# Residual rows of one panel put together in DRAM ahead of time, in a two-layer graph attention kernel

## The chip, the cores and the metric

The kernel runs on one core of a Trainium2 chip. The metric is the device time of one execution in microseconds (us); lower is better. The core has a matrix engine (TensorE, PE in the profile; its weight loads are PEld), a vector engine (VectorE, DVE), an activation engine (ScalarE, ACT), GpSimd (POOL) and a sync engine (SP). In this kernel SP issues nearly all loads from DRAM, and POOL issues the stores and those transfers that add to what is already at their destination. All transfers (DMAs) run on the same 16 DMA engines.

## What is computed

Two layers of graph attention over N = 2708 nodes with D = 1024 features, each with a layer norm ahead and a residual. Layer 0 is the one that the change touches:

```python
h = jnp.maximum(_layernorm(x, axis=-1), 0.0)
f = h @ Wf + bf;  g = h @ Wg + bg
e = relu(f @ g.T)
attention = softmax(where(adj > 0, e, NEG), axis=1)
x = x + attention @ (h @ W + bW)              # layer 0
h = jnp.maximum(_layernorm(x, axis=-1), 0.0)
x = x + layer1(h, adj, W1, a1, a2)            # layer 1, attention from two dot products
```

The rows of a softmax sum to one, so the bias `bW` can be added to the result: layer 0 ends with `x + bW + (attention @ h) @ W`. The kernel computes it in this order. `x + bW` is what is called the residual here. The output of layer 0 is called `x1`.

## The kernel before

The nodes are cut into five panels of some 512 columns (`NP = 5`), and each panel into four tiles of 128 rows (tiles 16 to 19 are panel 4; a few left-over rows have two tiles of their own in other panels). The rows of a tile are not contiguous in `x`: a tile takes four blocks of 32 rows that lie 128 rows apart, because of how masks are transposed (`places`). Matrix products are done by a scheme of seven half-size products (Strassen), called M1 to M7 in code and text.

For each panel of layer 0 four stages follow each other on PE:

- `project_q(p)`: the query side of the panel.
- `scores(p)`: for ten pairs of tiles (`for q in range(NQ)`, line 1403) seven products each, with one operand (`As`) streamed from DRAM; DVE evicts the results, turns the adjacency into masks and keeps row maxima. The masks are stored by POOL.
- `aggregate(0, p)`: attention times `h`, with `hc` streamed from DRAM.
- `project(0, p)`: the result times `W`, with `w` streamed from DRAM. For the last panel it runs pair by pair (`by_pair=True`, line 1705), in the order M1, M5, M2, M6, M7, M3, M4 for each of its two pairs of tiles, and each product of eight matmuls loads its own 1 MB of `w`.

`project` loads the weights of its first two products, then calls the `start` of `finish0(p)` (line 1218). For each tile, `start` loads the residual: two halves of 512 columns, each from four blocks of 32 rows (`load_rows_of`, line 278), so eight loads of 64 KB a tile. Then POOL adds the bias to each half by a DMA that accumulates (line 1612), with a source that repeats the same row 128 times. For panel 4, a mask is loaded as well for each tile (line 1600). When a product is evicted, `go` adds the residual to it, stores the row to `x1_d` (a DRAM tensor per tile, in tile order, that layer 1 reads), and when both halves are there `rows_done` starts layer 1's row work: layer norm, dot products, row maxima.

What sets the order. `load` keeps SP's loads in the order of the program (line 139), so a load that waits for a buffer or for room in flight holds up those after it. Loads go to rotating buffers: a pool of 12 (`strm`, for `w`, `hc`, `As`, raw adjacency) and one of 54 (`slot`, for residual halves, masks, scores). Two helpers interleave small work with PE's: `behind(us)` takes pieces from a list as PE's time allows, among them `put_quarters` (load `hq`, four DVE operations on each, store), which prepares layer 1 during the late part of layer 0. Instructions that are not held in order are arranged when the program is built.

The order at the end of layer 0 is: scores of panel 4, `project(0, 3)`, `aggregate(0, 4)`, `project(0, 4)`, then layer 1.

Of the kernel before, what the change touches and what calls it, by code (L numbers as in the profile page):

```python
# [12 lines left out]
OP = mybir.AluOpType  # L13
# [5 lines left out]
P = 128  # L19
W = 512  # L20
# [37 lines left out]
def kernel(  # L58
# [66 lines left out]
    def slot(name, shape=(P, WX), dt=FP):  # L125
        return slots.tile(list(shape), dt, tag="slot", name=name)
# [10 lines left out]
    def load(o, i):  # L137
        for a, b in in_16(o, i):
            tc.keep_in_program_order(nc.sync.dma_start(a, b))
# [102 lines left out]
    def row_halves(name, from_stream=False):  # L242
        return halves(stream(name)) if from_stream else [slot(name)[:, :W] for _ in range(2)]
# [1109 lines left out]
    def scores(p, B):  # L1353

        w = width[p]
        h = w // 2
        lo, hi = slice(0, h), slice(h, w)
        fetch, convert, turn = makers[p]
        rb = slot("rb")
        if p == 0:  # L1360
            spread(rb, columns_of(p, r_[:, first_col[p]:]))
        else:
            row_on_all(rb, r_d[p], p)
        acc = slot("acc")
        S = [None] * NT
        rates = (0.6, 1.0, 0.65, 0.65, 0.65)
        lefts = {}

        def product(q, m, ps, start):
            n, i = P, BY_SCORES.index(m)  # L1370
            if i % 2 == 0:
                t = stream("As", (P, 2, NH, P))
                lefts[q] = t
                k = min(2, 7 - i)
                load(t[:, :k].rearrange("p m c j -> p (m c j)"),
                     hs_d[q][:, i:i + k].rearrange("p m c j -> p (m c j)"))
            for c in range(NH):
                nc.tensor.matmul(ps[:n, :h], lefts[q][:, i % 2, c, :n], B[m][c // 2][:, c % 2, :h],  # L1378
                                 start=(start and c == 0), stop=(c == NH - 1), skip_group_check=True)

        def finish(q, s, k):

            n, mk = once(q, k), mk_sb[p, q]
            nc.vector.scalar_tensor_tensor(s[:, :w], s[:, :w], 0.0, mk[:, k, :w], op0=OP.max, op1=OP.add)
            if q == 0 and k == 0:
                nc.vector.tensor_copy(acc[:, :w], s[:, :w])
            else:
                nc.vector.tensor_tensor(acc[:n, :w], acc[:n, :w], s[:n, :w], OP.max)
            if q in known:
                raise_max(p, q, k, mk[:n, k, :w])  # L1390

        def last(q, sb, Z, m1):

            n = P
            product(q, M4, Z, False)
            add(sb[:n, lo], Z[:n, :h], m1[:n, lo])
            finish(q, sb, 1)
            mk_sb.pop((p, q))
            behind(rate, True)

        nc.hold = ("vector",)
        left_over = None
        for q in range(NQ):
            n = P
            make_until(q + 2)
            rate = 1.3 if NQ - 1 not in made else rates[p]
            if q + 2 <= LEFT:
                fetch(q + 2)
            sa, sb = slot("Sa"), slot("Sb")
            S[pairs[q][0]], S[pairs[q][1]] = sa, sb  # L1410
            X, Y, Z = (bank(f"s{k}") for k in "xyz")
            m1, t = slot("sm1"), slot("st")
            product(q, M1, X, True)
            for s in (lo, hi):
                add(m1[:n, s], X[:n, :h], rb[:n, s])
            if left_over:
                left_over()
            product(q, M6, Z, True)
            add(t[:n, lo], Z[:n, :h], m1[:n, hi])
            behind(rate, True)  # L1420
            product(q, M5, Y, True)
            add(t[:n, hi], Y[:n, :h], m1[:n, hi])
            if q + 1 <= LEFT:
                convert(q + 1)
            behind(rate, True)
            product(q, M2, X, False)
            add(sa[:n, lo], X[:n, :h], rb[:n, lo])
            if q + 1 <= LEFT:
                turn(q + 1, 0)
            behind(rate, True)  # L1430
            product(q, M7, Z, False)
            add(sb[:n, hi], Z[:n, :h], t[:n, hi])
            if q + 1 <= LEFT:
                turn(q + 1, 1)
            behind(rate, True)
            product(q, M3, Y, False)
            add(sa[:n, hi], Y[:n, :h], t[:n, lo])
            finish(q, sa, 0)
            behind(2 * rate, True)
            left_over = lambda q=q, sb=sb, Z=Z, m1=m1: last(q, sb, Z, m1)  # L1440

        sm, st = slot("Sa"), slot("Sb")
        S[MONO], S[TINY] = sm, st
        X, Y, Z = (bank(f"s{k}") for k in "xyz")
        m1, zs = slot("sm1"), slot("sz")
        t = stream("As", (P, 2, NH, P))
        load(t.rearrange("p e c j -> p (e c j)"), hsl_d.rearrange("p e c j -> p (e c j)"))

        def part(ps, e, m, start):
            for c in range(NH):  # L1450
                nc.tensor.matmul(ps[:, :h], t[:, e, c], B[m][c // 2][:, c % 2, :h], start=(start and c == 0),
                                 stop=(c == NH - 1), skip_group_check=True)
        part(X, 0, M1, True)
        add(m1[:, hi], X[:, :h], rb[:, hi])
        left_over()

        for c in range(NH):
            for g, (e, m) in enumerate(((0, M1), (1, M2), (0, M5), (1, M3))):
                nc.tensor.matmul(Z[B32 * g:B32 * (g + 1), :h], tinyT[:, e, c], B[m][c // 2][:, c % 2, :h], start=(c == 0),
                                 stop=(c == NH - 1), skip_group_check=True)  # L1460
        nc.scalar.copy(zs[:, :h], Z[:, :h])
        part(X, 1, M2, False)
        add(sm[:, lo], X[:, :h], rb[:, lo])
        behind(rate, True)
        part(Y, 0, M5, True)
        part(Y, 1, M3, False)
        add(sm[:, hi], Y[:, :h], m1[:, hi])
        finish(LEFT, sm, 0)
        for s, pick in zip((lo, hi), picks):
            V = bank("sv")  # L1470
            nc.tensor.matmul(V[:, :h], pick, zs[:, :h], start=True, stop=True)
            add(st[:, s], V[:, :h], rb[:, s])
        finish(LEFT, st, 1)
        mk_sb.pop((p, LEFT))
        behind(rate, True)
        nc.hold = ()
        return S, acc
# [113 lines left out]
    def bias_of_W(o, n, k):  # L1591
        return bass.AP(tensor=bw.tensor, offset=bw.offset + o, ap=[[0, n], [1, k]])

    def finish0(p):
        xs, seen = {}, {}

        def start(ts):
            for t in ts:
                if p == NP - 1:
                    first_mask[t] = load_mask(0, *pair_of[t])  # L1600
                if t == TINY:
                    xs[t] = halves_of_tiny("x_res")
                    for e in range(2):
                        for ps, i in by_quarters(x, places[TINY][0][1], e):
                            load(xs[t][e][ps], i)
                        for g, (ps, _) in enumerate(by_quarters(x, 0, e)):
                            nc.gpsimd.dma_start(xs[t][e][ps], bias_of_W(e * W + g * P, NY, P), accum_op=OP.add)
                    continue
                xs[t] = row_halves("x_res", t == MONO)
                load_rows_of(t, xs[t], x)  # L1610
                for e in range(2):
                    nc.gpsimd.dma_start(xs[t][e], bias_of_W(e * W, P, W), accum_op=OP.add)

        def go(t, e, c):
            add(xs[t][e], c, xs[t][e])
            if t == TINY:
                for ps, o in by_quarters(x1_d[t], 0, e):
                    store(o, xs[t][e][ps])
            else:
                store(x1_d[t][:, e * W:(e + 1) * W], xs[t][e])  # L1620
            seen[t] = seen.get(t, 0) + 1
            if seen[t] == 2 and t == TINY:
                put(0.5, lambda: rows_of_tiny())
            elif seen[t] == 2:
                rows_done(t, xs[t])

        def rows_of_tiny():
            xs[TINY] = row_halves("x_res")
            for e in range(2):
                nc.gpsimd.memset(xs[TINY][e], 0.0)  # L1630
                for ps, _ in places[TINY]:
                    nc.gpsimd.dma_start(xs[TINY][e][ps], x1_d[TINY][:, e * W:(e + 1) * W])
            rows_done(TINY, xs[TINY])

        def join(t, e, c):
            add(xs[t][e], xs[t][e], c)
        return start, join, go
# [199 lines left out]
```

## Time and profile before

| | us |
|---|---|
| median of 3 runs | 3094.57 |
| lowest and highest | 3094.34, 3098.68 |
| the profiled execution, whole | 3099.78 |
| its span, first to last instruction | 3098.0 |
| PE busy | 3002.8 (97%) |
| DVE busy | 2070.7 (67%) |
| POOL busy | 506.3 (16%) |
| ACT busy | 463.2 (15%) |
| mean granted clock of PE | 0.989 |

The profile describes one execution, with all its times counted from the start of the span. PE is busy nearly throughout, so the table says little of where time can be had; one has to look for the few places where PE waits or has a lower clock. In the span, the stages that the text speaks of lie at: scores of panel 4, 1771 to 1902; `project(0, 3)` from 1902; the end of `aggregate(0, 4)` (products M7 and M4, named `gz` and `gv` after their accumulators) 2044 to 2085; `project(0, 4)` (accumulators `px`, `py`, `pz`, `pv`) from 2085.15; layer 1's first long product from 2160.91. The residual halves appear as `x_res`, the source of the bias as `in_L_gnn_bW_dram`, `x1_d` as `x_d`, the reordered operands of layer 1 as `hq`, and masks loaded again from DRAM as `maskl`.

The DMA engines moved 764.70 MB, 247 GB/s over the span. SP's queue (q1) took 62.0% of the 16 engines' time, POOL's (q0) 16.4%.

### The profile page before, as it was taken

To read this page: it belongs to the slowest core of one execution; us is meant where nothing else is said; L and a number is where in the kernel's file an instruction comes from. 1 tells how busy PE (TensorE), PEld (TensorE's weight loads), DVE (VectorE), ACT (ScalarE), POOL (GpSimd) and SP (SyncE) were. 2 spreads that over 40 slices of the span, in tenths; PEclk is the share of its full clock that TensorE was granted. 3 is DMA by queue.
4 is the path that set the end of the run, shared out by engine and by line. 5 is a ranking of instruction groups with operands and counts; after the bars stand their busy time and mean duration, and the time that the engine had idled before them with its cause. 6 is when DMAs were issued, how large, how long until landed. Compare 5 with 4: busy or idle time off the path is not lost.

```text
span 3098.0 us, 41680 instructions
## 1 busy us (share of the span) xinstructions
PE 3002.8 (97%) x14630; PEld 2298.1 (74%) x14630; DVE 2070.7 (67%) x4615; ACT 463.2 (15%) x817; POOL 506.3 (16%) x786
## 2 busy tenths in 40 slices
PE   8998999899999999999999999997999999999998
PEld 4576777657877588885888886783777969879694
DVE  5767693776651596716975277766968768887853
ACT  3420020010110101101011001301222121212200
POOL 1421101310011110214101001141202010020202
PEclk9999999999999999999999999998999999999999
DMA  6999967998565796758967577789667868888896
GB/s 225 291 257 254 301 247 253 309 274 229 178 238 153 217 260 223 244 158 241 278 199 255 164 217 234 237 266 350 229 216 249 274 202 296 287 269 294 264 297 246
DMA packets 448577, 764.70 MB, mean 247 GB/s; under 512 B 175776, under 2 KB 262592, under 8 KB 448368
## 3 DMA queue, kind: packets, MB, share of 16 engines
q1 hardware_dynamic: 393008, 598.31, 62.0%
q0 software_dynamic: 55360, 163.73, 16.4%
q8 instruction: 116, 1.90, 0.3%
q14 instruction: 93, 0.76, 0.1%
HBM read 627.95 MB, written 133.91 MB: 246 GB/s over the span
## 4 chain that ended last, share of the span: by engine, by line
PE 71%; DVE 11%; DMA 7%; issue 7%; SPq 2%; POOL 1%; ACT 1%; POOLq 0%; DVEq 0%; ACTq 0%
PE sz L1378 6%; PE gx L661 6%; PE gy L661 6%; PE gz L661 5%; PE gz L1067 5%; PE pz L1267 4%; PE sx L1378 4%; PE sy L1378 4%; PE px L1267 4%; PE py L1267 3%; PE gx L1067 3%; PE gy L1067 3%; PE M_ps L574 3%; PE qz L661 2%; PE qx L661 2%
## 5 line engine op out<-in xcount | busy, mean ns | idle before, releaser
L1378 PE MATMUL sz<-B,As 128*128 128x288 f32 (+2 forms) x1200 | 293.5, 394 | 11.8 <-DVE st L45 8.8
L1378 PEld LDWEIGHTS sz<-B,As 128*128 128x128 f32 x1200 | 227.8, 191 | 61.8 <-DVE st L45 12.7
L1378 PE MATMUL sx<-B,As 128*128 128x288 f32 (+2 forms) x800 | 199.6, 392 | 6.4 <-DMA As<-hs_d 4.4
L1378 PE MATMUL sy<-B,As 128*128 128x288 f32 (+2 forms) x800 | 199.3, 392 | 2.3 <-DMA As<-hs_d 2.3
L661 PE MATMUL gz<-Sa,hc 128*128 128x288 f32 (+2 forms) x800 | 189.2, 397 | 6.3 <-DMA hc<-hg_d 6.3
L661 PEld LDWEIGHTS gz<-Sa,hc 128*128 128x128 f32 x800 | 153.8, 193 | 40.1 <-DMA hc<-hg_d 6.8
L1378 PEld LDWEIGHTS sx<-B,As 128*128 128x128 f32 x800 | 151.3, 190 | 40.1 <-DMA As<-hs_d 3.7
L1378 PEld LDWEIGHTS sy<-B,As 128*128 128x128 f32 x800 | 152.0, 190 | 33.4 <-issue 2.7
L1067 PE MATMUL gz<-quarter,hc 128*128 128x128 f32 (+2 forms) x1344 | 168.8, 279 | 3.8 <-DVE gT L45 3.7
L143 POOL DMA_DIRECT2D out_dram<-x_res x180 | 89.0, 501 | 482.1 <-DVE x_res L45 474.7
L1067 PEld LDWEIGHTS gz<-quarter,hc 128*128 128x128 f32 x1344 | 160.6, 191 | 5.1 <-DVE gT L45 4.6
L1267 PE MATMUL px<-w,gT 128*128 128x512 f32 x320 | 143.9, 602 | 7.5 <-DMA w<-in_L_gnn_W_dram 6.0
L1267 PE MATMUL pz<-w,ps 128*128 128x512 f32 x320 | 142.1, 594 | 0.8 <-DVE pt L45 0.8
L1267 PE MATMUL py<-w,ps 128*128 128x512 f32 x320 | 142.0, 593 | 0.0
L143 POOL DMA_DIRECT2D mk_d<-mask x55 | 35.8, 652 | 534.8 <-DVE mask L45 528.1
L1267 PEld LDWEIGHTS px<-w,gT 128*128 128x128 f32 x320 | 60.9, 193 | 80.9 <-issue 74.7
L1267 PEld LDWEIGHTS pz<-w,ps 128*128 128x128 f32 x320 | 60.2, 190 | 77.1 <-issue 70.7
L1267 PEld LDWEIGHTS py<-w,ps 128*128 128x128 f32 x320 | 60.5, 190 | 75.8 <-issue 73.9
L574 PE MATMUL M_ps<-wgT,wfT 128*128 128x512 f32 x256 | 113.5, 600 | 1.6 <-ACT hsT L45 1.6
L661 PE MATMUL gy<-T,hc 128*128 128x288 f32 (+2 forms) x480 | 111.6, 394 | 0.0
L977 POOL TENSOR_TENSOR gT<-gT,rr 128x2304 f32<-128x2304 f32 (+5 forms) x12 | 44.4, 3700 | 382.4 <-DVE rr L45 179.8
L661 PEld LDWEIGHTS gy<-T,hc 128*128 128x128 f32 x480 | 91.2, 190 | 19.5
(377 smaller groups left out, 5803.6 us busy)
## 6 DMA issues: line engine op xcount, KB each, us to landing
hc<-hg_d SPq DMA_DIRECT2D x175, 512.0 KB
As<-hs_d SPq DMA_DIRECT2D x150, 512.0 KB
hc<-hr_d SPq DMA_DIRECT2D x119, 512.0 KB
hc<-hs_d SPq DMA_DIRECT2D x112, 512.0 KB
w<-wt_d SPq DMA_DIRECT2D x96, 512.0 KB
w<-in_L_gnn_W_dram SPq DMA_DIRECT2D x72, 512.0 KB
md<-md_d SPq DMA_DIRECT2D x56, 512.0 KB
adj_i<-in_adj_dram SPq DMA_DIRECT2D x200, 128.0 KB
```

What stands on the lines that cost most here:

```text
L143: nc.gpsimd.dma_start(a, b)
L574: nc.tensor.matmul(ps, wfT[a][c // NH][:, c % NH, :], wgT[b][c], start=(c == 0), stop=(c == NC - 1))
L661: nc.tensor.matmul(ps[d], left(m, k, d), right(m, k), start=(start and k == 0), stop=(k == K - 1), skip_group_check=True)
L977: nc.gpsimd.tensor_tensor(of(e, s), of(e, s), by(s, k), OP.mult)
L1067: nc.tensor.matmul(ps[:, d], lhs[:, d * P:(d + 1) * P], inner_right(m, n, k), start=(start and k == 0 and d == 0), stop=(k == NK - 1), ski ...
L1267: nc.tensor.matmul(ps, left[i][m][:, k, :], w_[k], start=(start and k == 0), stop=(k == NH - 1), skip_group_check=True)
L1378: nc.tensor.matmul(ps[:n, :h], lefts[q][:, i % 2, c, :n], B[m][c // 2][:, c % 2, :h], start=(start and c == 0), stop=(c == NH - 1), skip_g ...
```

## The change

For panel 4 alone the residual is put together in DRAM during the scores of panel 4, some 300 us ahead of its use, and in the order of the tile. At pair 2 POOL issues four DMAs that copy the rows of `x` for tiles 16 to 19 into `x1_d`, DRAM to DRAM, 512 KB each, with the source as 4 groups of 32 rows. At pair 6 it issues four accumulating DMAs of 512 KB that add the bias row to all 128 rows of each tile in DRAM. In `project(0, 4)`, `start` then has two loads of 128 x 512 a tile from `x1_d` in place of eight loads and two accumulating DMAs. The later stores to `x1_d` are as before, over the same rows.

```diff
@@ -1406,6 +1406,8 @@
             if q + 2 <= LEFT:
                 fetch(q + 2)
+            if p in ORDERED and q in (2, 6):
+                (copy_residual if q == 2 else bias_residual)(p)
             sa, sb = slot("Sa"), slot("Sb")
@@ -1591,6 +1593,30 @@
+    def tiles_of(p):
+        return list(full(p)) + ([MONO, TINY][p - 1:p] if p in (1, 2) else [])
+
+    ORDERED = (NP - 1,)
+
+    def by_gpsimd(o, i, **k):
+        tc.keep_in_program_order(nc.gpsimd.dma_start(o, i, **k))
+
+    def copy_residual(p):
+        for t in tiles_of(p):
+            if t < MONO:
+                r = places[t][0][1]
+                by_gpsimd(x1_d[t].rearrange("(g r) c -> g r c", g=P // B32),
+                                    bass.AP(tensor=x.tensor, offset=x.offset + r * D, ap=[[P * D, P // B32], [D, B32], [1, D]]))
...
+
+    def bias_residual(p):
+        for t in tiles_of(p):
+            n = NY if t == TINY else P
+            by_gpsimd(x1_d[t], bass.AP(tensor=bw.tensor, offset=bw.offset, ap=[[0, n], [1, D]]), accum_op=OP.add)
+
@@ -1607,6 +1633,10 @@
                 xs[t] = row_halves("x_res", t == MONO)
+                if p in ORDERED:
+                    for e in range(2):
+                        load(xs[t][e], x1_d[t][:, e * W:(e + 1) * W])
+                    continue
                 load_rows_of(t, xs[t], x)
                 for e in range(2):
                     nc.gpsimd.dma_start(xs[t][e], bias_of_W(e * W, P, W), accum_op=OP.add)
```

The new POOL DMAs are held in program order on POOL; the loads from `x1_d` go through `load` and so keep their place on SP.

## The prediction

> **What bounds the kernel now.** I read the page first: TensorE (PE) is busy 97% of the 3098.0 us span, so only a place where PE stands idle or runs slowly can pay. Among the costly groups one line has a transfer behind its idle time:
>
> ```profile
> L1267 PE MATMUL px<-w,gT 128*128 128x512 f32 x320 | 143.9, 602 | 7.5 <-DMA w<-in_L_gnn_W_dram 6.0
> ```
>
> Its last columns are the idle time before these matmuls, 7.5 us, of which 6.0 ended with a load of weights `w`. I looked for those 6 us in the timeline of PE and found them in the last projection of layer 0, where the touched `finish0(4)` is in use:
>
> ```profile
> 2088.59 3.60 PE L1267 MATMUL py<-w,ps 128*128 128x512 f32 x8
> 2098.14 6.29 PE L1267 MATMUL px<-w,gT 128*128 128x512 f32 x8 [5.96 <-DMA w<-in_L_gnn_W_dram]
> 2104.27 3.60 PE L1267 MATMUL pz<-w,ps 128*128 128x512 f32 x8
> ```
>
> Columns: start, extent, what, idle time before and what ended it. PE stops for 5.96 us, and the next eight matmuls take 6.29 us instead of 3.60. Why `w` is late stands in the timeline of SP, which issues all loads in program order:
>
> ```profile
> 2054.56 2.82 SPq L139 DMA_DIRECT2D w<-wt_d  x2
> 2057.47 1.45 SPq L139 DMA_DIRECT2D maskl<-mk_d  x1
> 2058.97 7.89 SPq L139 DMA_DIRECT2D x_res<-in_x_dram  x8
> 2067.05 0.34 SPq L139 DMA_DIRECT2D maskl<-mk_d  x1
> 2067.84 5.95 SPq L139 DMA_DIRECT2D x_res<-in_x_dram  x8
> ...
> 2080.83 7.90 SPq L139 DMA_DIRECT2D x_res<-in_x_dram  x8
> 2088.77 1.82 SPq L139 DMA_DIRECT2D w<-in_L_gnn_W_dram  x2
> ```
>
> Between the weights of the second product (M5) and of the third (M2) stand 32 loads of 64 KB, the residual rows of panel 4. They hold SP from 2058.97 to 2088.73; M2's weights leave at 2088.77 and PE needs them at 2092.19. The bias then gets in their way: GpSimd (POOL) adds it by eight accumulating transfers.
>
> ```profile
> 2082.09 5.38 POOL L1612 DMA_DIRECT2D x_res<-in_L_gnn_bW_dram  x6
> 2089.75 0.86 POOL L1612 DMA_DIRECT2D x_res<-in_L_gnn_bW_dram  x1 [2.28 <-DMA x_res<-in_x_dram]
> 2095.24 0.86 POOL L1612 DMA_DIRECT2D x_res<-in_L_gnn_bW_dram  x1 [4.63 <-DMA x_res<-in_x_dram]
> ```
>
> The table by windows shows the DMA engines full (share 1.13 in 2089 to 2093, 1.09 in 2093 to 2098) at only 226 and 261 GB/s, against 402 in 2105 to 2120 without them. M2's weights, 1 MB, take 9.2 us.
>
> **What the Trainium skill says.** Its page "DMA: Bandwidth & Descriptors", section "Rules for kernel authors", calls small transfers mostly overhead and says to coalesce them. The trace agrees in kind: SP waits for an earlier `x_res` load to land 16 times, 6.6 us, in this stretch, so few bytes are in flight. The same page, "Queues, rings and completion order", says that each DMA engine takes turns between queues packet by packet. The trace agrees: in 2059 to 2067 POOL's queue moved 595 packets and SP's 492. "TensorE: Matmul & The Clock Gate", Part 1, halves the clock after an idle window of about 3.4 us; here the granted clock is 0.61 in 2098 to 2105. The DMA page again, "Why a DMA increments its semaphore by 16 and not by 1", says that a DMA takes as many engines as divide the slowest dimension of both sides: the new copies have a slowest dimension of 4, so perhaps 4 engines. No run here shows that yet.
>
> **The change part by part.**
>
> *SP in the last projection.* 32 loads of 64 KB become 8 of 256 KB; the four mask loads and the bytes (2 MB) stay. Alone, 12 issues would take some 12 x 0.4 = 5 us (an issue takes 0.31 to 0.42 when nothing holds it). But landing limits them: SP's queue moved 1.02 MB in 2059 to 2067, 126 GB/s, beside POOL's. At that rate 2 MB + 0.6 MB of masks take 21 us, and M2's weights leave at about 2080 at the latest. At the same rate 1 MB takes 8 us: 2088, and POOL's other traffic ends at 2083, which makes it earlier. Needed at 2092.2: margin 4 us or more. Their buffers hold no load back: the stream pool has 12, M2's two were last read by the M7 products, over at 2065. M6, M7 and M3 follow as the `gv` products free buffers (2068 to 2085), each before its use.
>
> *What goes.* PE idles 5.96 us less. The eight slow matmuls go from 6.13 us start to start (2098.14 to 2104.27) to 3.44: 2.69 less. Sum 8.65 us. The eight accumulates go from this stretch too; they held over half of the DMA engines (56.6% for POOL's queue in 2089 to 2105), about 9 us of the whole set there. That pays for the compression of the stage: from 2092 on PE takes 1 MB of weights per 3.44 us, 305 GB/s, which the 402 GB/s of 2105 to 2140 cover with stores and masks beside it.
>
> *What is late next.* VectorE's (DVE) eviction of M6 before M7 accumulates on it, 0.78 us at 2107.9, stays. After the stage the path is DVE's (layer norm, dots, row maxima; PE waits 8.33 us at 2151.58 for `mx`). It starts with the last products, so it moves forward whole. A hidden gain: DVE's 2.45 us wait for the bias at 2092.21 goes, worth nothing because PE stood.
>
> *What is added in scores 4.* Four DRAM to DRAM copies of 512 KB at pair 2, four accumulates of 512 KB at pair 6. On POOL: 8 instructions of 0.7 to 2.2 us (stores 0.73, accumulates 0.84 to 2.25), behind them only mask stores, one per 12.09 us, for which nobody waits in this stage. The accumulates wait for the copies, issued four pairs (48 us) earlier. Cost on POOL: nothing; uncovered, at most 16 us of POOL alone.
>
> On the DMA engines: the trace has no DRAM to DRAM transfer. From below nothing, since the engines are busy 0.65 to 0.82 here and PE never waits for `As`. From above: the eight accumulates of panel 3 were issued in 1890.9 to 1902.2 and the slowest landed in 15.8 us, so 2 MB took at most 27 us; twice that, 54 us, for DRAM on both sides. I take nothing, because loads run ahead:
>
> ```profile
> 1742.09 6.34 SPq L139 DMA_DIRECT2D As<-hs_d  x3
> 1771.20 1.89 PE L1378 MATMUL sx<-B,As 128*128 128x256 f32 x8
> ```
>
> The first `As` is issued 29 us ahead of its use; SP waits for PE to free buffers, so the lead persists, and a burst has to delay loads by over 20 us to be seen. The later `x_res` loads wait for accumulates about 200 us old: nothing.
>
> *Sum.* -8.65 + 0 = -8.6 us. The profiled execution took 3099.78 us (span 3098.0 and 1.8 around it); it would take 3091.2. It lies 5.2 above the median of the runs, so I put the difference on the median: 3094.57 - 8.6 = 3086.0.
>
> **The rivals.**
>
> *A, the stall goes:* 3086.0; its own range 3083 to 3088.3.
>
> *B, a new wait takes part of its place.* Bigger loads put more packets of SP beside POOL's `hq` loads, for which DVE already waits in turn (four waits, 6.0 us; PE lost 0.97 us at 2064.98 behind it). Those four waits grown by half are 3 us, and a wait for M6's or M7's weights at full rings could be 1 to 2. Against it: POOL's queue is free after 2083. Saving 4: 3090.6.
>
> *C, slower: the DRAM accumulates are slow.* Place: from pair 6 (issued about 1842) to the projection of panel 3. Its own bias accumulates are issued at 1890.9 on the same queue, and DVE uses the first at 1912.84. The point: 2 MB must take longer than about 54 us, twice the measured bound, so that they end after 1896 and push panel 3's 27 us past 1912.84. At three times the bound (81 us, end 1923) panel 3's bias lands up to 27 us later; DVE and PE stop some 20, and 2.7 more go to the clock: 3094.57 - 8.65 + 22.7 = 3108.6. For it: accumulates already ran at half speed. Against: four transfers can overlap.
>
> *D, the order of issue shifts.* Only held instructions keep program order; the others are put in order at build time by expected readiness, which changes here. Place: the DVE chain of 2138 to 2160, where each half dot costs 0.76 us (0.68 and 0.08). Twelve of them ahead of the maxima cost 9.1 and end the gain: 3095.1.
>
> *E, it does more.* The 9 us of freed DMA time also shorten other waits: 3081.
>
> **How the numbers follow.** Chances: A 0.48, B 0.18, C 0.07, D 0.22, E 0.05. I can tell 0.2%, 6.2 us, from no change: the bounds are 3088.4 and 3100.8. A, less 0.03 for its edge, and E lie below: faster 0.50. B, that edge and the lighter third of D (0.08) lie between: same 0.29. C and the rest of D (0.14), which has no bound in the trace and which I spread up to 15 us over its 3095.1, lie above: slower 0.21. The predicted time is A's, 3086.0. The range goes from 3082, which leaves out E, to 3103, which leaves out C and half of D's slower part (0.07): 0.19 outside.
>
> **What would show it.** Right: SP shows 8 `x_res` loads before M2's weights, issued by 2080 on the old clock; PE has no idle time before the third product and its matmuls take 0.43 us each; POOL has no L1612 there; scores 4 still spans 130.7 us (1771.2 to 1901.9). Wrong: a wait for `As` or `x_res` at 1840 to 1915 (C), a longer wait for `hq` (B), or a longer way from the last product to the first of layer 1 than the 17.7 us of now (2143.25 to 2160.91, D).

## The result and the profile after

| | before | after |
|---|---|---|
| median of 20 runs each, same chip, us | 3095.03 | 3087.0 |
| lowest and highest, us | 3092.05, 3104.18 | 3081.28, 3097.34 |
| the profiled execution, us | 3099.78 | 3084.88 |
| its span, us | 3098.0 | 3083.0 |
| data moved, MB | 764.70 | 766.79 |

The ratio is 0.9972, 95% interval 0.9964 to 0.998: 8.7 us less, 6.2 to 11.1; the two medians differ by 8.0. In the page's costliest groups, the line that led to the stall now reads (columns as before: busy time, mean ns, idle time before):

```profile
L1267 PE MATMUL px<-w,gT 128*128 128x512 f32 x320 | 141.2, 593 | 1.5 <-ACT pt L45 1.5
```

The 6.0 us behind a load of `w` are gone, and the busy time is 2.7 us lower, since the eight matmuls at the low clock are gone too. PE's timeline after, where the last projection begins (start, extent, what):

```profile
2083.55 3.60 PE L1267 MATMUL py<-w,ps 128*128 128x512 f32 x8
2086.98 3.60 PE L1267 MATMUL px<-w,gT 128*128 128x512 f32 x8
2090.41 3.60 PE L1267 MATMUL pz<-w,ps 128*128 128x512 f32 x8
2093.85 1.02 PE L1267 MATMUL py<-w,ps 128*128 128x512 f32 x2
2094.80 3.70 PE L1267 MATMUL pz<-w,ps 128*128 128x512 f32 x8
```

The second line is M2: no idle time, 3.60 us. Two matmuls of M3 now stand between M6 and M7 (the fourth line) and fill the 0.78 us in which PE waited for DVE there. SP's timeline after, in the same stretch:

```profile
2049.54 2.82 SPq L139 DMA_DIRECT2D w<-wt_d  x2
...
2053.99 1.35 SPq L139 DMA_DIRECT2D x_res<-x_d  x2
...
2066.21 1.15 SPq L139 DMA_DIRECT2D x_res<-x_d  x2
...
2068.89 2.33 SPq L139 DMA_DIRECT2D w<-in_L_gnn_W_dram  x2
```

Eight loads of 256 KB in pairs, the last at 2066.21, and M2's weights leave at 2068.89, 18 us before their use. The last column of the table by windows, after, is GB/s; the one ahead of it is the busy share of the DMA engines:

```profile
2084.00:2088.00 4.00, 4.00 (x11) 1.85 (x10) 2.11 (x5) 0.34 (x1) 0.00 (x0) 1.00 1.03 407
2088.00:2093.00 5.00, 5.00 (x14) 2.13 (x13) 1.99 (x3) 0.00 (x0) 0.57 (x1) 1.00 1.04 397
```

Before, while `w` was late, the same columns read:

```profile
2089.00:2093.00 4.00, 3.18 (x8) 1.14 (x6) 1.55 (x4) 0.37 (x1) 0.86 (x1) 1.00 1.13 226
2093.00:2098.00 5.00, 0.00 (x0) 0.00 (x0) 1.20 (x2) 0.00 (x0) 0.86 (x1) 0.86 1.09 261
```

The engines are as full as before, but carry 400 GB/s in place of 226 to 261.

The spans differ by 15.0 us, which is more than the change brought. By stages: 5.23 us lie ahead of the change's first instruction (scores of panel 4 begin at 1765.97, before 1771.20), mostly in small waits of the first 600 us, which the change does not touch; the profiled execution of before lay 5 us above its median. Scores of panel 4: 130.70 to 130.91, 0.21 longer. `project(0, 3)` with `aggregate(0, 4)`: 183.25 and 183.23. `project(0, 4)`, from its first product's start to its last product's: 54.50 to 44.83, 9.67 shorter (5.96 + 2.69 + 0.78 for the M6 wait, 0.24 left unexplained). From the end of that last product to the first long product of layer 1: the same 17.7 us. The remaining 0.3 us lie in layer 1. So the change's own places give 9.67 - 0.21 = 9.5 us, within the interval of the timed runs.

### The profile page after: what moved, and what is told of

The parts are those of the page before. It is cut to its first block, busy times and chain, and to the rows that moved or that the text cites. A ratio compares the mean times of both kernels' runs of the same rounds, so it can differ in the third digit from the quotient of the medians.

```text
span 3083.0 us, 41611 instructions
## 1 busy us (share of the span) xinstructions
PE 3000.3 (97%) x14630; PEld 2299.3 (75%) x14630; DVE 2069.9 (67%) x4615; ACT 460.9 (15%) x815; POOL 504.1 (16%) x786
## 2 busy tenths in 40 slices
DMA packets 447808, 766.79 MB, mean 249 GB/s; under 512 B 175488, under 2 KB 262304, under 8 KB 447568
## 4 chain that ended last, share of the span: by engine, by line
PE 74%; DVE 11%; issue 7%; DMA 5%; POOL 1%; SPq 1%; ACT 1%; POOLq 0%; DVEq 0%; ACTq 0%
PE sz L1378 6%; PE gx L661 6%; PE gy L661 6%; PE gz L661 5%; PE gz L1067 5%; PE sx L1378 4%; PE pz L1267 4%; PE px L1267 4%; PE sy L1378 4%; PE py L1267 3%; PE gy L1067 3%; PE gx L1067 3%; PE gv L661 3%; PE M_ps L574 3%; PE qz L661 2%
```

## Experiments

The open question was the cause of the stall. The change does two things at once in the last projection: SP issues 8 loads in place of 32, and POOL's eight accumulates are gone. And it adds 4 MB of written data in an earlier stage, which the timed result can't price. "Project" below is the same stretch of `project(0, 4)` as above: 54.50 us before, 44.83 after. All ratios are to the kernel before, beside it on the same chip.

| run | ratio, 95% interval | project, us |
|---|---|---|
| e1_copy_only | 0.9994, 0.9985 to 1.0002 | 53.51 |
| e2_small_loads | 0.9970, 0.9962 to 0.9978 | 45.69 |
| e3_split | 1.0007, 0.9998 to 1.0015 | 59.32 |
| e4_dram_work_alone | 1.0003, 0.9993 to 1.0012 | 54.24 |
| e5_plain_broadcast | 0.9993, 0.9985 to 1.0002 | 50.32 |
| e6_distinct_rows | 0.9997, 0.9988 to 1.0006 | 55.39 |
| e7_no_bias | 0.9973, 0.9965 to 0.9982 | 45.69 |
| e8_three_doses | 1.0064, 1.0049 to 1.0078 | 44.82 |
| e9_copy_plain | 0.9976, 0.9966 to 0.9985 | 44.88 |
| e10_spread | 0.9962, 0.9951 to 0.9973 | 44.83 |
| e11_two_panels | 1.0027, 1.0017 to 1.0037 | 44.83 |
| e12_two_spread | 0.9986, 0.9979 to 0.9993 | 44.82 |

### e1_copy_only: only the loads coalesced

The copies stay at pair 2; the accumulates stay in the last projection, on POOL.

```diff
-            if p in ORDERED and q in (2, 6):
-                (copy_residual if q == 2 else bias_residual)(p)
+            if p in ORDERED and q == 2:
+                copy_residual(p)
...
                     for e in range(2):
                         load(xs[t][e], x1_d[t][:, e * W:(e + 1) * W])
-                    continue
-                load_rows_of(t, xs[t], x)
+                else:
+                    load_rows_of(t, xs[t], x)
```

> Copies into x1_d at pair 2 as in the change and two loads of 256 KB a half tile row block from there, but the bias is added in the on-chip tiles by eight accumulating DMAs in the last projection, as before. Theory S (the third product's weights were late because SP stood behind 32 small loads): they leave SP some 15 us earlier, PE's 5.96 us wait and the 2.7 us of low clock go, 8 to 9 us below before. Rival T (the accumulates, which hold over half of the DMA engines, made them late): most of the wait stays, at most 3 us below before.

Measured: 0.9994, no gain that can be told. SP issues M2's weights early, in its timeline:

```profile
2072.43 2.30 SPq L139 DMA_DIRECT2D w<-in_L_gnn_W_dram  x2
```

and still PE stops, two products later. PE's timeline of the same run:

```profile
2093.57 3.60 PE L1267 MATMUL pz<-w,ps 128*128 128x512 f32 x8
2102.99 2.05 PE L1267 MATMUL py<-w,ps 128*128 128x512 f32 x2 [5.82 <-DMA w<-in_L_gnn_W_dram]
```

These matmuls are M3's. Its weights left SP at 2080.68, 22 us before, and landed as PE resumed. The accumulates were issued from 2080.21 to 2088.96, and this is the table by windows while they run:

```profile
2091.27:2095.27 4.00, 4.00 (x10) 1.72 (x9) 0.29 (x1) 0.00 (x0) 0.00 (x0) 1.00 1.09 273
2095.27:2099.27 4.00, 1.90 (x5) 0.57 (x3) 3.10 (x6) 0.00 (x0) 0.55 (x1) 1.00 1.09 270
```

A full share at 270 GB/s, much as before. SP's order alone does not make the stall: with the order mended, it moved to later weights.

### e2_small_loads: only the accumulates moved

All is as in the changed kernel, but the residual comes from `x1_d` in 32 loads of 64 KB, as many as before.

```diff
-                        load(xs[t][e], x1_d[t][:, e * W:(e + 1) * W])
+                        for ps, _ in places[t]:
+                            load(xs[t][e][ps], x1_d[t][ps, e * W:(e + 1) * W])
```

> Residual and bias put together in DRAM as in the change, no accumulate in the last projection, but fetched from there by 32 loads of 64 KB. Theory S: SP still stands behind the 32 loads until about 3 us before PE needs the third product's weights; without the accumulates these land in 3 to 5 us and not 9.2, so PE waits 0 to 3 us: 5 to 8 us below before. Rival T: all of the gain, and M2's weights in time however late they leave: 8 to 9 us below before, with no wait of PE.

Measured: 0.997, the whole gain. SP's timeline:

```profile
2077.16 5.20 SPq L139 DMA_DIRECT2D x_res<-x_d  x8
2082.41 0.94 SPq L139 DMA_DIRECT2D w<-in_L_gnn_W_dram  x2
```

PE's timeline:

```profile
2088.52 3.60 PE L1267 MATMUL px<-w,gT 128*128 128x512 f32 x8
```

M2's weights leave 6.1 us before their use, behind the same 32 loads, and arrive in time. In the kernel before they left 3.4 us before their use and needed 9.2. The M6 wait of 0.78 us is there again, which is most of what e2's stretch is longer than the changed kernel's. This pair of runs takes the two halves of the change apart: the coalesced loads alone bring nothing, the moved accumulates alone bring everything.

### e3_split: the second pair's residual asked for later

In the kernel before, the second pair's loads (and so its four accumulates) are put after the first pair's M6.

```diff
+        in_two = l == 0 and by_pair
-        start_of([t for g in todo for t in g[:2]] + ([other] if other else []))
+        start_of(list(todo[0][:2]) if in_two else [t for g in todo for t in g[:2]] + ([other] if other else []))
...
+                if in_two and m == M6 and j + 1 < len(todo):
+                    start_of(list(todo[j + 1][:2]))
```

> The kernel before with no work in DRAM: the residual rows of the second pair of tiles are asked for after the first pair's fourth product, so that 16 small loads and not 32 stand ahead of the third product's weights; all eight accumulates stay in the last projection. Theory S: weights leave SP at about 2074 on the clock of before, wait and low clock go: 8 to 9 us below before. Rival T: the accumulates still hold the engines: at most 3 us below before.

Measured: 1.0007. M2 has no wait any more, but six others have come, of 0.34 to 4.40 us, 9.9 in sum. The longest, in PE's timeline:

```profile
2124.00 4.41 PE L1268 MATMUL pz<-w,ps 128*128 128x512 f32 x6 [4.40 <-DMA w<-wt_d]
```

This run does not tell the two causes apart, since it moves both. Sixteen small loads now hold SP ahead of M7's weights, which leave at 2091.99 and are wanted at 2093.98; and four accumulates, issued from 2095.12, lie beside the weights of the second pair. It shows that asking for the second pair later, within the projection, gains nothing.

### e4_dram_work_alone: the added work without the benefit

The copies and the four large accumulates go into tensors that nobody reads; the last projection is that of before.

```diff
+    spare_d = {t: dram.tile([P, D], FP, name=f"spare_d{t}") for t in full(NP - 1)}
...
-                by_gpsimd(x1_d[t].rearrange("(g r) c -> g r c", g=P // B32),
+                by_gpsimd(spare_d[t].rearrange("(g r) c -> g r c", g=P // B32),
-            by_gpsimd(x1_d[t], bass.AP(...), accum_op=OP.add)
+            by_gpsimd(spare_d[t], bass.AP(...), accum_op=OP.add)
...
-                if p in ORDERED:
-                    for e in range(2):
-                        load(xs[t][e], x1_d[t][:, e * W:(e + 1) * W])
-                    continue
```

> The kernel before plus the four copies and four accumulates in DRAM during the scores of panel 4, into tensors that nobody reads. Theory S: hidden by the loads that run ahead, 0 to 0.5 us above before, with SP held for some 15 us after pair 6 and no wait of PE for As. Rival (the added work has a price that the measured gain already contains): 2 to 5 us above before.

Measured: 1.0003, interval 0.9993 to 1.0012, so the work costs between -2 and 4 us; the profile shows no wait for `As`, and the old stall at M2 (6.66 us). The work is hidden, as closely as this can be told: the interval does not rule out its rival's 2 to 4 us, but no wait in the profile would account for them.

### e5, e6 and e7: what it is in the accumulates

Three edits of the kernel before, for panel 4 alone: a plain DMA of the same bytes in place of the accumulate (e5), an accumulate of zeros from 128 different rows in place of one row repeated (e6), and no bias DMA at all (e7).

```diff
 e5
+     if p == NP - 1:
+         nc.gpsimd.dma_start(xs[t][e], bias_of_W(e * W, P, W))
+     else:
          nc.gpsimd.dma_start(xs[t][e], bias_of_W(e * W, P, W), accum_op=OP.add)
 e6
+ zero_d = dram.tile([P, W], FP, name="zero_d")
...
+     nc.gpsimd.dma_start(xs[t][e], zero_d if p == NP - 1 else bias_of_W(e * W, P, W), accum_op=OP.add)
 e7
+     if p < NP - 1:
          nc.gpsimd.dma_start(xs[t][e], bias_of_W(e * W, P, W), accum_op=OP.add)
```

> The kernel before, but for panel 4 the eight bias DMAs of the last projection overwrite the residual in place of adding to it: the same bytes from the same repeated row, at the same time, without the accumulate. It leaves the residual x out of panel 4's rows. Theory R (the source that repeats one row 128 times makes these transfers slow): the wait for weights stays, within 2 us of before. Theory C (the accumulate itself makes them slow): most of the wait goes, 6 to 9 us below before.

> The kernel before, but for panel 4 the eight accumulating DMAs read 128 distinct rows of a DRAM tensor of zeros in place of one repeated row. It leaves the bias out of panel 4. Theory R: the transfers run at the rate of other loads, the wait for weights goes, 6 to 9 us below before. Theory C: the accumulate costs what it did, within 2 us of before.

> The kernel before with the eight bias DMAs of the last projection left out (the bias is not added in panel 4), and no work in DRAM; the 32 small loads stay. It is the bound for every way of taking the accumulates away: 8 to 9 us below before. If the work in DRAM during the scores has a price of its own, this lies below the changed kernel by that price; expected 0 to 1 us.

Measured. e7, 0.9973: M2's weights left SP 6.6 us before their use, and PE did not wait. First SP's timeline, then PE's:

```profile
2085.84 0.94 SPq L139 DMA_DIRECT2D w<-in_L_gnn_W_dram  x2
2092.40 3.60 PE L1267 MATMUL px<-w,gT 128*128 128x512 f32 x8
```

This is the bound on what moving the bias can bring, and the changed kernel reaches it. e6, 0.9997: the stall is there in full, in PE's timeline:

```profile
2096.51 6.41 PE L1268 MATMUL px<-w,gT 128*128 128x512 f32 x8 [6.73 <-DMA w<-in_L_gnn_W_dram]
```

and the windows of e6 have the low rate at a full share:

```profile
2086.00:2090.00 4.00, 3.78 (x9) 1.33 (x7) 1.62 (x4) 0.58 (x1) 0.86 (x1) 1.00 1.12 227
2090.00:2094.00 4.00, 0.00 (x0) 0.00 (x0) 1.73 (x3) 0.00 (x0) 0.81 (x1) 1.00 1.10 262
```

So the repeated source row is not what makes them slow. e5, 0.9993: half of the wait remains (and one of 1.00 us comes later), in PE's timeline:

```profile
2092.81 3.92 PE L1267 MATMUL px<-w,gT 128*128 128x512 f32 x8 [2.92 <-DMA w<-in_L_gnn_W_dram]
```

Its weights left SP at 2084.14, behind the 32 loads and 5.75 us before they were wanted. The project stretch is 4.2 us shorter than before, but no gain shows in the timed runs, whose interval ends at 0.9985, 4.6 us; neither expectation was fully met. Plain bytes at that place still cost something where the weights leave late.

### e9_copy_plain: coalesced loads and a plain bias

e1 with e5's edit: the weights leave early, the bias moves the same bytes at the same place, and only the accumulation is missing.

```diff
 (on top of e1)
-                    nc.gpsimd.dma_start(xs[t][e], bias_of_W(e * W, P, W), accum_op=OP.add)
+                    if p == NP - 1:
+                        nc.gpsimd.dma_start(xs[t][e], bias_of_W(e * W, P, W))
+                    else:
+                        nc.gpsimd.dma_start(xs[t][e], bias_of_W(e * W, P, W), accum_op=OP.add)
```

> The run with copies alone (8 large loads from x1_d, bias DMAs in the last projection), but these bias DMAs overwrite in place of adding, for panel 4; it leaves the residual x out of panel 4's rows. If the accumulate is what fills the DMA engines and the late issue on SP only decides where it is felt, weights that leave early and no accumulate together give all of the gain, 7 to 9 us below before, with under 1 us of waiting for weights in the last projection. If 2 MB of any transfer there is too much, at least 3 us of waiting stays and it is at most 5 us below before.

Measured: 0.9976, project 44.88, no wait. The table by windows, while the bias moves:

```profile
2083.34:2087.34 4.00, 4.00 (x11) 1.84 (x10) 3.62 (x6) 0.36 (x1) 1.57 (x3) 1.00 1.03 412
2087.34:2091.34 4.00, 4.00 (x11) 1.77 (x10) 0.75 (x3) 0.23 (x1) 0.54 (x1) 1.00 1.04 372
```

Against e1's 273 and 270 GB/s, with the accumulation as the only difference of the two programs. That the transfers accumulate is what costs e1 its gain. Beside e5, which has the same plain bias, this run differs by the eight large loads (and the copies they read): there coalescing took the last waits away, 50.32 to 44.88 us.

### e8_three_doses: how much of the added work is hidden

Eight more accumulates of 512 KB at pair 6 of panel 4 (12 in place of 4), into tensors of their own that are cleared during scores of panel 3.

```diff
+        for i in range(2):
+            for t in range(F):
+                by_gpsimd(spare_d[i][t], bass.AP(...), accum_op=OP.add)
```

> The changed kernel with twice as much again added at pair 6: eight more accumulates of 512 KB in DRAM, into tensors that nobody reads (cleared by 16 stores in the scores of panel 3). If one dose of 2 MB takes 18 us of full DMA engines and hides behind loads that run 29 us ahead, three take some 54 us, the lead is used up, and PE waits for As or for panel 3's residual 10 to 30 us: 2 to 22 us above before. If accumulates in DRAM are cheap beside other loads, PE does not wait and it stays at the changed kernel's time.

Measured: 1.0064; by the two ratios 28.5 us above the changed kernel ((1.0064 - 0.9972) x 3095). Scores of panel 4 take 160.44 us in place of 130.91. SP's timeline of e8:

```profile
1840.93 44.94 SPq L139 DMA_DIRECT2D adj_i<-in_adj_dram  x8
```

PE's timeline of e8:

```profile
1892.48 3.78 PE L1378 MATMUL sx<-B,As 128*128 128x256 f32 x8 [27.41 <-DMA As<-hs_d]
```

The work that costs next to nothing in one dose stops PE for 27.41 us in three. The place shows in the changed kernel too. Its SP timeline at pair 6:

```profile
1836.96 19.58 SPq L139 DMA_DIRECT2D adj_i<-in_adj_dram  x8
1856.63 4.29 SPq L139 DMA_DIRECT2D As<-hs_d  x8
```

In the kernel before, the same eight loads of raw adjacency held SP for 5.14 us:

```profile
1842.19 5.14 SPq L139 DMA_DIRECT2D adj_i<-in_adj_dram  x8
```

In the changed kernel, in 1838 to 1856, POOL's queue took 84.2% of the DMA engines for 2.62 MB, and SP's 15.0% for 0.34 MB. So the `As` behind them left 14.4 us later, and the first was needed at 1861.04. Timeline of PE's weight loads, after:

```profile
1861.04 1.59 PEld L1378 LDWEIGHTS sx<-B,As 128*128 128x128 f32 x8 [0.34 <-DMA As<-hs_d]
```

The idle time ahead of it, 0.34 us, ended with `As`; between the groups before and after it there are 0.02 to 0.03 us. The stage is 0.21 us longer than before. So the cover was used up, and a little more.

### e10_spread: the accumulates apart

One large accumulate at each of the pairs 4 to 7, in place of four at pair 6.

```diff
+            if p in ORDERED and q == 2:
+                copy_residual(p)
+            if p in ORDERED and 4 <= q < 8:
+                bias_residual(p, [full(p)[q - 4]])
...
+    def bias_residual(p, ts):
+        for t in ts:
```

> The changed kernel with its four accumulates in DRAM issued one a pair, at pairs 4 to 7, and not all at pair 6. The loads of the scores stage should be held some 4 us at a time in place of 14 at once, so that As lands well ahead of use. If the one dose at pair 6 sometimes makes PE wait (its As landed just in time in the profile), this is 0.5 to 3 us below the changed kernel; if it never does, the same within 0.5 us.

Measured: 0.9962, interval 0.9951 to 0.9973; scores of panel 4 take 130.70 us, as before the change. SP's timeline:

```profile
1840.56 8.81 SPq L139 DMA_DIRECT2D adj_i<-in_adj_dram  x8
1849.47 11.47 SPq L139 DMA_DIRECT2D As<-hs_d  x8
```

SP is held for 8.81 us in place of 19.58. The ratio is the lowest of all, but its interval overlaps that of the changed kernel (0.9964 to 0.998): that it is faster isn't shown, that the cover is back is.

### e11_two_panels and e12_two_spread: panel 3 as well

e11 does the same for panels 3 and 4; e12 does so with e10's spreading.

```diff
-    ORDERED = (NP - 1,)
+    ORDERED = (NP - 2, NP - 1)
```

> The change for panels 3 and 4. In the projection of panel 3 PE never waits for weights, so taking its accumulates away gains nothing; the added work in the scores of panel 3 is hidden as narrowly as in panel 4. Expected at the changed kernel's time, within 1 us; if the added work there is not hidden, up to 5 us above it; if DMA time matters on its own, wherever it is freed, 3 us or more below it.

> Panels 3 and 4 as in the run before, but with one accumulate in DRAM a pair at pairs 4 to 7 of each panel's scores. If the loss there was the burst of four at pair 6 (11.33 us of PE waiting for As in the scores of panel 3), it goes: no wait of over 1 us for As, and the time of the run with one panel spread, within 2 us (0.995 to 0.997 of before). If the amount of added DMA work is what does not fit into the scores of panel 3, at least 5 us of waiting for As stay and it is at 0.998 or above.

Measured: e11 1.0027, some 17 us above the changed kernel where at most 5 were expected: missed. Scores of panel 3, up to the first product with the left-over rows, take 143.51 us in place of 129.75. PE's timeline of e11:

```profile
1551.34 3.78 PE L1378 MATMUL sx<-B,As 128*128 128x256 f32 x8 [11.33 <-DMA As<-hs_d]
```

The same burst, at panel 3's pair 6, is not covered there. e12 came between its expectations, its ratio in the range of the second and its waits in neither: 0.9986, and scores of panel 3 take 131.51 by the same count. PE's timeline of e12:

```profile
1527.28 1.99 PE L1378 MATMUL sx<-B,As 128*128 128x256 f32 x8 [1.84 <-DMA As<-hs_d]
```

Spreading takes most of the wait away. Yet e12 stays 7 us above e10 by the ratios, give or take 4, of which the stage explains 1.8. In the profiled executions, 3.8 us more lie behind the last product of the program, where the last stores land (17.8 us to the end in e11 and e12, 14.0 in e10); but it is 17.1 in e7, which adds no work in DRAM, so this is not shown to come from panel 3's. Where the rest goes stays open.

## Why the prediction was right, and where it was not

**The total.** Forecast 8.6 us less, measured 8.7 (6.2 to 11.1), and a median of 3087.0 for 3086.0. Case A held: PE's wait before the third product and the eight slow matmuls went, 5.96 + 2.69 us as summed.

**Why `w` was late: the step that failed.** The prediction read the cause from SP's order: 32 loads hold SP, so M2's weights leave late. It let the accumulates only "get in their way". The runs turn this round. With the order mended and the accumulates left, no gain can be told and the stall moves to M3 (e1). With the order left and the accumulates gone, all is gained (e2, e7). Both sums give 8.6 because both causes go in the change, so the agreement of the total says nothing on which it was. Here luck helped: for e1, which only mends the order, the same reasoning promised 8 to 9 us.

What carries the stall is DMA time: beside the accumulates the engines are full at 226 to 295 GB/s. In the trace's records of single packets, e1's eight accumulates are 1024 packets of 2048 bytes at 0.176 us (median), and a plain load's packet of that size took 0.085 us in the same stretch. Over 16 engines that is 11.26 us against 5.44. The difference, 5.8 us, is an estimate from these medians; PE's stall was 5.96 us in the kernel before and 5.82 in e1. The prediction had quoted some 9 us of the DMA set for the accumulates, from a stretch that held only part of them, but did not make it the cause.

The late issue was in part the accumulates' own doing: with the same 32 loads and no accumulates, M2's weights left 6.6 us before their use (e7) in place of 3.4. By itself it has a part only where other transfers stand in the way: with plain bytes it leaves 2.92 us (e5), with plain bytes and early weights none (e9).

**M2's weights "leave at about 2080".** They left at 2068.89, which is 2074 on the old clock: the loads were not limited by the 126 GB/s read from 2059 to 2067. In that stretch the engines were full, with 66.9% of their time on POOL's queue and 34.7% on SP's, so the rate is what POOL's transfers left. It shows no price of small loads, though the prediction read SP's 16 waits that way. It did no harm, as it erred on the safe side.

**Turns by packet.** The near-equal counts of 2059 to 2067 (595 and 492) are not general here: in 1838 to 1856 of the changed kernel SP's queue moved 2759 packets and POOL's 734, and it was SP that was held. Whether the copies ran on four engines each, no view shows; they landed in 9.3 us (median).

**The M6 wait of 0.78 us "stays".** It stayed in e2 and e7. In the changed kernel (and in e9) two matmuls of M3 fill it, so case D, the order of issue shifts, occurred here with a small gain, while the DVE chain it was feared for did not change: 17.7 us from the last product, as "moves forward whole" said.

**Added DRAM work at nothing.** Right in its outcome (e4, and the changed kernel's ratio is e7's within the noise), mis-sized in its cover. "A burst has to delay loads by over 20 us to be seen" took the lead of 29 us from the start of the stage. At pair 6 the burst delayed `As` by 14.4 us and the stage had already lost 0.2, so the cover at that place is some 14 us. The burst itself fits the bound: the four accumulates landed in 16.8 us (median), under the 27. Case C stayed away. Its point, 54 us until panel 3's bias is late, was not reached in any run. In e8 SP was held for 44.94 us and PE waited 27.41 us for `As`, while nothing waited for that bias: the first wait is for `As`, and it comes earlier.

**Rival B.** Its wait for `hq` didn't grow: four waits, 6.0 us before, 6.1 after. **E** was not needed for the result.

## What to carry to other kernels

A late load has two candidate causes, when it was issued and how long it took to land, and a change that removes both proves neither: undo one half at a time. Where the DMA engines are full at a low rate, ask which transfer takes their time; here moving accumulating transfers to a stage with spare DMA time was worth it, and coalescing loads was not, neither beside the accumulates (e1) nor without them (e2); it paid only beside plain bias bytes (e5 against e9). Read the cover for such a burst from the lead of the loads at the very place it is put, and spread the burst if it comes near to that lead.

## What the runs showed of the hardware

- An accumulating DMA into on-chip memory took about twice the engine time of a plain one of the same bytes: 0.176 us for a packet of 2048 bytes against 0.085 (medians, e1); POOL's plain packets of 4096 bytes took 0.160 (e9). While eight of 256 KB ran, the full engines moved 227 to 295 GB/s (e1, e6), against 372 to 412 with the same transfers plain (e9). The profile counts an accumulate's bytes once: with 2 MB of copies added and the accumulates only moved elsewhere, the data moved grew by 2.09 MB. Landing took 10.3 to 18.4 us in e1 and 9.1 to 10.3 in e9; issuing one took POOL 0.84 us against 0.54. Whether the source row is repeated or 128 rows differ made no difference (e6).
- Four accumulates of 512 KB with DRAM on both sides landed in 16.8 us (median), and the whole core moved 165 GB/s meanwhile; the copies of 512 KB landed in 9.3 us (median).
- Beside such accumulates the queue with small packets got 15.0% of the engines' time: eight 64 KB adjacency loads, whose packets are under 512 bytes, held SP for 19.58 us in place of 5.14, and for 44.94 with three doses (e8).
- Coalescing, which the Trainium skill ("DMA: Bandwidth & Descriptors", section "Rules for kernel authors") advises, gave nothing that can be measured beside the accumulates (e1) or without them: 32 loads of 64 KB in e2 came to 0.997, eight of 256 KB in the changed kernel to 0.9972. The section speaks of transfers under 64 KB as mostly overhead; these had just 64 KB. M2's weights left SP 18.1 us before their use in place of 6.1, and PE had no use for the difference.
